# The passage from three attention layers to a state space layer: banks, load order and diagonals

## The chip, the cores and the metric

The kernel runs on one core of one Trainium2 chip. The metric is the device time of one launch in microseconds (us), the median of several runs. Engines are named as in the profile: PE (TensorE matmul) and PEld (its weight loads), DVE (VectorE), ACT (ScalarE), POOL (GpSimd), and SP (SyncE), which here issues nearly all DMAs.

## The reference

Four layers run one after the other over x of shape (8, 512, 256), all conditioned by `cond`. Layers 0 to 2 are transformer blocks (attention and an MLP). Layer 3 is a bidirectional state space layer with a gated MLP. Cut to the part that matters:

```python
def _mamba(h, ...):
    x, z = jnp.split(h @ in_proj_W, 2, axis=-1)              # 512 channels each
    x = silu(causal_conv(x, conv_w) + conv_b)                # 4 taps per channel
    xdbl = x @ x_proj_W                                      # 16 + 32 + 32 columns
    dt = softplus(xdbl[..., :16] @ dt_proj_W + dt_proj_b)
    Bm, Cm = xdbl[..., 16:48], xdbl[..., 48:]
    A = -jnp.exp(A_log)
    # for each time t, for 512 channels x 32 states:
    #   hst = hst * exp(dt_t * A) + dt_t * B_t * x_t ;   y_t = sum_n hst * C_t
    return (ys + Dp * x) * silu(z) @ out_proj_W
h = ln(x) * (1 + s1) + sh1
x = x + g1 * (mamba(h) + flip(mamba(flip(h))))
x = x + g2 * (silu(h2 @ w1) * (h2 @ w2) @ w3)                # h2: the second norm of x
```

All data is float32.

## The kernel before

The activations are kept transposed: 128 channels on the partitions, 512 time steps along the free axis. Layers 0 to 2 share one set of pools and hand their results over through DRAM (`x_mid`). When their pools close, those of layer 3 open in the same memory.

Every engine's order of work is the order in which the Python code emits it. Each engine takes its own list in order and waits with semaphores, so the order written by hand is the schedule.

**Layer 3** makes 16 steps: for each of 8 batch items a forward and a reversed pass. A step's preparation is `prep3`; a step's recurrence is `recur`, 64 turns k of 32 channels by 8 states (c = k // 16 is the channel block, gp = k % 16 // 4 the pair of state groups, j = k % 4). In a turn:

- `fill(k)` (L1190, PE): 64 small products of the transposed inputs `ut` with the diagonal matrices `dg` write one `bx` tile, two PSUM banks wide. There are three `bx` tiles, which take six of the eight banks; one bank each goes to `bank` and to `yc`.
- `decay(k)` (L1165, ACT): two exponentials into `da`, of which there are four (`N_DA`). They read `dtr`, the step size of 32 channels copied to four groups of partitions.
- `scan(k)` (L1204, DVE): two scans of 128x512. After each second turn POOL multiplies by `cs` (L1208), and PE sums over the states into `yc` (L1229 to L1236).

The preparation of later steps is interleaved with the turns by credits. The preparation of the first step has nothing beside it: `run_interleaved(prep3(*steps[0]))`. It runs through these places, all of which put PE's products into the one `bank` tile:

- `norm3`: mean (L883) and variance (L892), with DVE, ACT and POOL work between (L885, L888, L893, L895, L897, L900).
- four products with `w_x0` (L861), copied out by ACT (L954);
- `convolve`: four times three products (L930), finished by DVE (L937), then a silu on ACT (L964);
- the product with `w_x` (L971), copied out twice (L973, L975); transposes (L982) to `bt` (L986);
- four products with `w_dt` (L996), each copied out by ACT (L999); one softplus (L1002);
- `dt` goes to DRAM in `dt_s` (L1005), from where `spread` (L1115) fetches `dtr`; C goes through `c_s`, from where `spread_c` (L1123) fetches `cs`;
- four times: a POOL product `uc` (L1011; one buffer), four transposes (L1019), a copy to `ut` (L1023).

After it come `spread_c` and `diagonal` for all four gp. A diagonal of one s is 8 ACT instructions (L1138) or one POOL instruction (L1142), after `DIAG = "AAPA"`. Only then `recur` begins, which first calls `spread` for four q.

The setup ahead of `prep3` loads `w_x`, `w_dt`, four pieces of `a_log` (made into `negA` on ACT, L818), `w_x0` (`fetch`, L797) and last the input `hz` (L877).

Of the kernel before, what the change touches and what calls it, by code (L numbers as in the profile page):

```python
# [7 lines left out]
F32 = mybir.dt.float32  # L8
# [6 lines left out]
B, L, D = 8, 512, 256  # L15
N_STATE, D_IN, DT_RANK = 32, 512, 16
# [12 lines left out]
SUMS_LATE, DIAG, STAGGER, RATE, CREDIT = 3, "AAPA", 2, 4.0, 4.0  # L29
# [38 lines left out]
def run_interleaved(*gens):  # L68
    live = list(gens)
    while live:  # L70
        live = [g for g in live if next(g, "end") != "end"]
# [3 lines left out]
def dit_mamba_kernel(ctx: ExitStack, tc: tile.TileContext, t, out):  # L75
    nc = tc.nc
# [13 lines left out]
    def vcol(name, i):  # L90
# [6 lines left out]
    x_mid = {  # L97
        (l, b): dram.tile([D, L], F32, tag=f"xm{l}_{b}", name="x_mid") for l in range(3) for b in range(B)
    }
# [20 lines left out]
    with ExitStack() as actx:  # L120
# [4 lines left out]
        def bank():  # L125
            return ps.tile([128, L], F32, tag="s", name="s", bufs=7)
# [645 lines left out]
    with ExitStack() as mctx:  # L772
        mp_ = mctx.enter_context(tc.tile_pool(name="mp", bufs=1))
        scr = mctx.enter_context(tc.tile_pool(name="scr", bufs=2, space=bass.MemoryType.DRAM))
        ps_m = mctx.enter_context(tc.tile_pool(name="ps_m", bufs=1, space=PSUM))

        def bank():
            return ps_m.tile([128, L], F32, tag="bank", name="bank")

        order = ["w_x0"]
# [4 lines left out]
        def fetch(name, tag="wp", bufs=1):  # L787
            w = mp_.tile([128, 1024], F32, tag=tag, name="w", bufs=bufs)
            if name in ("w_x0", "w_z0"):
                src, k = t["w_in"].rearrange("(k p) m -> p k m", p=128), 2  # L790
                src = src[:, :, 0:D_IN] if name == "w_x0" else src[:, :, D_IN:]
            else:
                k = t[name].shape[0] // 128
                src = t[name].rearrange("(k p) m -> p k m", p=128)
            m = src.shape[-1]
            ring[name] = w[:, 0 : k * m].rearrange("p (k m) -> p k m", k=k)
            nc.sync.dma_start(ring[name], src)  # L797
# [9 lines left out]
                fetch(order[0])  # L807

        w_x = mp_.tile([128, 4, 80], F32, tag="w_x", name="w_x")
        nc.sync.dma_start(w_x, t["w_x"].rearrange("(k p) m -> p k m", p=128))  # L810
        w_dt = mp_.tile([80, D_IN], F32, tag="w_dt", name="w_dt")
        nc.sync.dma_start(w_dt[64:80, :], t["w_dt"])
        negA = mp_.tile([128, N_Q, N_G], F32, tag="negA", name="negA")
        a_log = mp_.tile([128, N_Q, N_STATE], F32, tag="ut", name="a_log", bufs=N_UT)
# [24 lines left out]
        xp = mp_.tile([128, 4, L + 6], F32, tag="xp", name="xp")  # L839
        nc.vector.memset(xp[:, :, 0:3], 0.0)  # L840
        nc.vector.memset(xp[:, :, L + 3 : L + 6], 0.0)
        fetch(order[0])


        WAIT, LAST, ALONE = -1, 100, 200
        st = {}
        n_p = N_G // 2
        n_k = N_Q * n_p

# [5 lines left out]
        def dense(w, src, n_k, c):  # L855

            p = yield from free_bank()
            for k in range(n_k):
                if k == 2:
                    yield 2  # L860
                nc.tensor.matmul(  # L861
                    p, w[:, k, c * 128 : (c + 1) * 128], src[:, k, :], start=k == 0, stop=k == n_k - 1
                )
            return p

        def free_bank():
            while held[0]:
                yield WAIT
            held[0] = True
            return bank()  # L870

        def taken():
            held[0] = False

        def load_x3(b, tag):
            x = st[tag, b] = mp_.tile([128, 2, L], F32, tag=tag, name=tag)
            nc.sync.dma_start(x, x_mid[2, b].rearrange("(k p) n -> p k n", p=128))  # L877

        def norm3(x, h, sq, r, sc, sh):

# [61 lines left out]
        def prep3(b, rev):  # L942

            if not rev:
# [7 lines left out]
                for c in range(4):  # L952
                    p = yield from dense(w, h, 2, c)
# [13 lines left out]
            p = yield from free_bank()  # L967
# [12 lines left out]
            p = yield from free_bank()  # L980
# [10 lines left out]
            dt_s = scr.tile([D_IN, L], F32, tag="dt", name="dt_s")  # L991
            st["in", b, rev] = us, uts, dt_s, c_s
            dt = mp_.tile([128, 4, L], F32, tag="dt", name="dt")
            for c in range(4):
                p = yield from free_bank()
# [6 lines left out]
            nc.scalar.activation(dt, dt, AF.Softplus)  # L1002
            use_exp_ln(pin=False)
            yield ALONE
            nc.sync.dma_start(dt_s.rearrange("(c p) t -> p c t", p=128), dt)  # L1005
            st["dt", b, rev] = True

            def transposed(c):
# [19 lines left out]
            live, c, i = [], 0, 0  # L1028
            while live or c < 4:
# [4 lines left out]
                for g in list(live):  # L1034
                    n = next(g, None)
                    while n == WAIT:
                        yield WAIT
                        n = next(g, None)
# [62 lines left out]
        def later(turns, fn):  # L1101
            todo.append([turns, fn])
            todo.sort(key=lambda e: e[0])
# [3 lines left out]
        def spread(step, q):  # L1107

            if (step, q) in dtr:
                return  # L1110
            dt_s = st[("in",) + step][2]
            rt = mp_.tile([128, L], F32, tag="dtr", name="dtr", bufs=N_DT)
            src = dt_s[32 * q : 32 * q + 32, :]
            for n in range(4):
                nc.sync.dma_start(rt[32 * n : 32 * n + 32, :], src)  # L1115
            dtr[step, q] = rt

        def spread_c(step, gp):

            w = mp_.tile([128, 2, L], F32, tag="cs", name="cs", bufs=n_p)  # L1120
            src = st[("in",) + step][3].rearrange("(g n) t -> n g t", n=4)
            for n in range(4):
                nc.sync.dma_start(  # L1123
                    w[32 * n : 32 * n + 32, :, :],
                    src[n : n + 1, 2 * gp : 2 * gp + 2, :].to_broadcast([32, 2, L]),
                )
            cs[step, gp] = w

        def diagonal(step, gp, s):

            if s == 0:
                dg[step, gp] = mp_.tile([128, 4, 4, 64, 2], F32, tag="dg", name="dg", bufs=n_p)
            o = dg[step, gp][:, s]
            bt = st[("bt",) + step][:, s, 8 * gp : 8 * gp + 8]
            if DIAG[s] == "A":
                for i in range(2):
                    for n in range(4):
                        nc.scalar.activation(  # L1138
                            o[:, n, :, i], eye, AF.Copy, scale=bt[:, 4 * i + n : 4 * i + n + 1]
                        )  # L1140
            else:
                (nc.vector if DIAG[s] == "V" else nc.gpsimd).tensor_tensor(  # L1142
                    o, eye[:, None, :, None].to_broadcast([128, 4, 64, 2]),
                    bt.rearrange("p (i n) -> p n i", i=2)[:, :, None, :].to_broadcast([128, 4, 64, 2]),
                    ALU.mult,
                )
# [22 lines left out]
        def recur(step, nxt, ys):  # L1169
# [75 lines left out]
            for k in range(n_k):  # L1245
                c, gp, j = k // 16, k % 16 // 4, k % 4
                run_due(1)
                if k % 2 == 0:
                    fill(k)
                    fill(k + 1)  # L1250
                    for i in range(0 if k else -AHEAD, 2):
                        decay(step, nxt, k + AHEAD + i)
                n_ut[1] += k % 16 == 15
                later(2, lambda k=k: scan(k))
                if j == 3:
                    later(2 + SUMS_LATE, lambda c=c, gp=gp: sums(c, gp))
                    if c == 3 and nxt:
                        for s in range(4):
                            later(1 + 3 * s, lambda gp=gp, s=s: diagonal(nxt, gp, s))
                        later(4, lambda gp=gp: spread_c(nxt, gp))  # L1260
                if k % 16 in SPREAD:
                    i = SPREAD.index(k % 16)
                    if c < 3:
                        spread(step, 4 * (c + 1) + i)
                    elif nxt and ("dt",) + nxt in st:
                        spread(nxt, i)
                yield k
# [9 lines left out]
        steps = [(b, rev) for b in range(B) for rev in (False, True)]  # L1277

        def before(step):

            b, rev = step
            if rev:
                conv = convolve(b, True)
                if b:

                    for _ in range(6):
                        yield next(conv)
                    while (b - 1, True) not in done:
                        yield WAIT
                yield from conv  # L1290
                yield from gates(b)
                if b + 1 < B:
                    load_x3(b + 1, "hz")
            yield from prep3(b, rev)

        def behind(b, ys):

            while (b, True) not in done:
                yield WAIT
            yield from project(b, ys)  # L1300

            yield from mlp3(b, ys[:, 2:4, :])
            
            if b + 1 < B:
                load_x3(b + 1, "x")
                fetch("w_out", "wq", 1)

        load_x3(0, "hz")
        run_interleaved(prep3(*steps[0]))
        for gp in range(n_p):  # L1310
            spread_c(steps[0], gp)
            for s in range(4):
                diagonal(steps[0], gp, s)
        ys = mp_.tile([128, 4, L], F32, tag="ys", name="ys")
        load_x3(0, "x")
        fetch("w_out", "wq", 1)
# [1 line left out]
        for i, step in enumerate(steps):  # L1318
            b, rev = step
# [137 lines left out]
```

## Time and profile before

| | |
|---|---|
| median of three runs | 6478.48 us (6462.92, 6478.48, 6481.08) |
| the profiled execution | 6473.94 us |
| its span, first to last instruction | 6472.1 us |
| busy share of the span | PE 90%, DVE 64%, POOL 57%, ACT 54% |
| mean granted TensorE clock | 0.959 |
| last store of layer 2 (L748) issued | 3455.11 us after the span's start |
| first product of layer 3 (L883) | 3467.19 us |
| first decay, first scan | 3564.09 us, 3564.82 us |

In timeline rows the columns are start (us), length (us), engine, line, operation, output and inputs, shape, count, and in brackets the idle time of the engine ahead and what ended it. Several instructions are merged into one row. A float32 product of 128x512 is two PE rows, called passes here.

### The profile page before, as it was taken

The page shows a single profiled execution, that of the slowest core. Times are in us where ns is not written, and L with a number is a line of the kernel's source. Part 1 is how long each engine was busy: PE and PEld are TensorE (multiplying, and loading weights), DVE is VectorE, ACT ScalarE, POOL GpSimd, SP SyncE. Part 2 cuts the span into 40 slices and gives each one's busy share as a digit, 9 for nine tenths or more (in the row PEclk, how much of TensorE's full clock was granted, in tenths as well). Part 3 has the DMA queues.
Part 4 walks back from the last instruction along what each step waited for, and adds up shares of the span by engine and source line. Part 5 has one row for each costly group of instructions (what it writes and reads, how often), then busy time and mean ns, then how long its engine had stood idle before and what let it go on. Part 6 is the DMA issues. An engine that isn't in the chain of part 4 may idle for free.

```text
span 6472.1 us, 200572 instructions
## 1 busy us (share of the span) xinstructions
PE 5842.6 (90%) x88928; PEld 2917.0 (45%) x88928; DVE 4110.2 (64%) x5102; ACT 3513.7 (54%) x6855; POOL 3665.9 (57%) x1464
## 2 busy tenths in 40 slices
PE   8999999999999989999995888988888888888887
PEld 4333335555555544333332444444444444444443
DVE  4554545544554544455531887888878888888886
ACT  2444444333433433444443677777777677777773
POOL 1110126655556662111001888888989888988896
PEclk8999999999999999999997999999999999999999
DMA  2001101000000000101001111112121211111120
GB/s 86 24 25 28 32 21 37 24 27 27 17 27 27 27 14 24 41 26 26 24 12 51 39 49 54 58 56 62 52 65 51 67 43 59 60 53 57 49 64 24
DMA packets 168559, 260.31 MB, mean 40 GB/s; under 512 B 40448, under 2 KB 58368, under 8 KB 167696
## 3 DMA queue, kind: packets, MB, share of 16 engines
q1 hardware_dynamic: 167152, 246.44, 12.5%
q8 instruction: 702, 11.50, 0.7%
q14 instruction: 161, 1.32, 0.1%
q10 hardware_dynamic: 544, 1.05, 0.0%
HBM read 186.53 MB, written 34.60 MB: 34 GB/s over the span
## 4 chain that ended last, share of the span: by engine, by line
PE 68%; ACT 10%; POOL 9%; DVE 6%; issue 5%; DMA 1%; SPq 1%; POOLq 0%; DVEq 0%; ACTq 0%
PE s L381 10%; PE s L674 8%; PE bx L1190 8%; POOL hs L1208 5%; PE bank L861 5%; PE s L637 5%; PE s L587 5%; PE yc L1236 5%; DVE hs L1204 4%; PE o L607 3%; PE s L498 3%; PE o L538 3%; ACT da L1165 3%; PE s L528 3%; PE bank L930 3%
## 5 line engine op out<-in xcount | busy, mean ns | idle before, releaser
L1204 DVE TENSOR_TENSOR_SCAN hs<-da,bx 128x512 f32<-128x512 f32 x2048 | 2311.1, 1198 | 425.3 <-ACT da L1165 245.7
L1208 POOL TENSOR_TENSOR hs<-hs,cs 128x2048 f32<-128x2048 f32 x512 | 2323.7, 4564 | 278.1 <-DVE hs L1204 201.7
L1165 ACT ACTIVATE da<-dtr,negA 128x512 f32<-128x512 f32 x2048 | 1335.4, 713 | 260.6 <-DVE hs L1204 247.9
L1190 PE MATMUL bx<-dg,ut 64*32 64x128 f32 x65536 | 1123.4, 276 | 249.1 <-DVE hs L1204 154.3
L1190 PEld LDWEIGHTS bx<-dg,ut 64*32 64x32 f32 x65536 | 941.8, 107 | 655.9 <-issue 473.9
L519 POOL TENSOR_SCALAR pr<-pr,sums 128x512 f32<-128x512 f32 x512 | 796.5, 1575 | 571.2 <-DVE sums L517 570.7
L592 DVE TENSOR_REDUCE negp<-s 128x1 f32<-128x512 f32 x1024 | 637.6, 683 | 586.7 <-PE s L587 586.2
L643 ACT ACTIVATE pt<-s 128x512 f32<-128x512 f32 x1024 | 527.7, 601 | 440.4 <-PE s L637 440.3
L1236 PE MATMUL yc<-hs,r 128*32 128x512 f32 x4096 | 608.1, 637 | 82.4 <-POOL hs L1208 81.4
L510 ACT ACTIVATE pr<-s,negm 128x512 f32<-128x512 f32 x512 | 345.1, 686 | 300.1 <-DVE negm L509 286.5
L529 DVE COPY pt<-s 128x512 f32<-128x512 f32 x512 | 321.6, 683 | 192.2 <-PE s L528 178.5
L509 DVE TENSOR_REDUCE negm<-s 128x1 f32<-128x512 f32 x512 | 317.4, 682 | 142.3 <-PE s L498 142.2
L587 PE MATMUL s<-kT,qT 32*128 32x512 f32 x2048 | 368.7, 653 | 36.1 <-ACT pt L643 18.2
L674 PE MATMUL s<-g,w_w 128*128 128x512 f32 x768 | 361.7, 617 | 23.9 <-ACT g L738 14.6
L1138 ACT ACTIVATE dg<-eye,bt 128x64 f32<-128x64 f32 x1536 | 381.3, 342 | 0.3 <-PE bx L1190 0.3
L353 POOL TENSOR_TENSOR xs<-x 128x512 f32<-128x512 f32 x48 | 61.0, 1272 | 564.1 <-DVE x L663 181.6
L381 PE MATMUL s<-h,w_w 128*128 128x512 f32 x768 | 366.5, 618 | 13.9 <-POOL h L372 13.9
L381 PE MATMUL s<-h,wqkv 128*128 128x512 f32 x768 | 368.3, 615 | 4.9 <-POOL h L372 4.7
L700 POOL COPY wide<-rec 128x1024 f32<-128x1024 f32 x16 | 16.6, 1037 | 622.9 <-DVE rec L698 622.9
L637 PE MATMUL s<-q,kT 32*128 32x512 f32 x2048 | 366.3, 649 | 1.8 <-DVE qs L454 1.4
L1236 PEld LDWEIGHTS yc<-hs,r 128*32 128x32 f32 x4096 | 126.7, 113 | 459.9 <-issue 297.9
L528 PE MATMUL s<-base,pr 128*128 128x128 f32 x2048 | 263.7, 279 | 42.9 <-POOL pr L519 37.9
(166 smaller groups left out, 6265.2 us busy)
## 6 DMA issues: line engine op xcount, KB each, us to landing
dtr<-dt_s SPq DMA_DIRECT2D x1024, 64.0 KB
cs<-c_s SPq DMA_DIRECT2D x256, 128.0 KB
wqkv<-in_wqkv_dram SPq DMA_DIRECT2D x48, 512.0 KB
dt_s<-dt SPq DMA_DIRECT2D x16, 1024.0 KB
x_mid<-x SPq DMA_DIRECT2D x24, 512.0 KB
x<-x_mid SPq DMA_DIRECT2D x24, 512.0 KB
w<-in_w_g_dram SPq DMA_DIRECT2D x24, 384.0 KB
qT<-qs SPq DMA_DIRECT2D x256, 32.0 KB
```

Of the source, the lines that this page charges most:

```text
L381: nc.tensor.matmul(p, w[:, k, o : o + 128], src[:, k, :], start=k == 0, stop=k == n - 1)
L519: nc.gpsimd.tensor_scalar(p[:, j, :], p[:, j, :], sums[:, j : j + 1], None, ALU.mult)
L587: nc.tensor.matmul(ss[j], u.qT[r, c, qt * 128 : (qt + 1) * 128], u.kT[r, c, :], start=True, stop=True)
L592: nc.vector.tensor_reduce(negp[c % 2][:, qt, i : i + 1], ss[j], AX.X, ALU.max, negate=True)
L637: nc.tensor.matmul(ss[j], u.kT[r, c, i * 128 : (i + 1) * 128], q2[u, c][r, :], start=True, stop=True)
L643: nc.scalar.activation(pt[j // 2][:, j % 2, :], ss[j], AF.Exp)
L674: nc.tensor.matmul(p, w[:, first + c, m * 128 : (m + 1) * 128], srcs[c], start=c == 0, stop=c == n - 1)
L1165: nc.scalar.activation(da[:, i, :], dtr[step, 4 * c + j], AF.Exp, scale=negA[:, 4 * c + j, g : g + 1])
L1190: nc.tensor.matmul(bx[k][32 * n : 32 * n + 32, r, 128 * s : 128 * s + 128], uts[c][64 * r : 64 * r + 64, s, 32 * j : 32 * j + 32], d[64 * ...
L1204: nc.vector.tensor_tensor_scan(h, back(da[:, i, :]), back(x[:, i, :]), 0.0, ALU.mult, ALU.add)
L1208: nc.gpsimd.tensor_tensor(hs[t_], hs[t_], cs[step, k % 16 // 4][:, None, :, :].to_broadcast([128, 2, 2, L]), ALU.mult,)
L1236: nc.tensor.matmul(yc[c][32 * j : 32 * j + 32, :], r32, h[j // 2][:, j % 2, i, :], start=False, stop=gp == n_p - 1 and i == 1, tile_positi ...
```

## The change

It touches four things, all in the passage from layer 2 to the first recurrence step, and leaves all instructions after the first ten turns in their order.

1. While the first preparation is alone, `bank()` hands out the first half of a `bx` tile, three in turn, in place of the one `bank` tile.
2. The first input `hz` and then `w_x0` are the first DMAs of layer 3; `w_x`, `w_dt` and `a_log` follow.
3. `dt` of the first step goes to DRAM in four pieces, and the 16 DMAs of `dtr` are issued ahead of the 16 of `cs` instead of behind them.
4. The diagonals of the first gp are made by DVE (s = 0, 2) and ACT (s = 1, 3); those of the other three gp keep `DIAG`, but are emitted during turns 0 to 9 instead of ahead of the recurrence.

In each engine's list before and after: ACT had 96 diagonal instructions, then decays; it now has 32, the decays of turns 0 and 1, 8, two turns of decays, 16, two turns, 8, two turns, 16, two turns, 8. POOL's four diagonals become three, between its multiplications. DVE has two more instructions, ahead of its first scan. ACT's four `negA` instructions now stand between those of the norm: one ahead of L888, two ahead of L893, one ahead of L900.

```diff
+        alone = [True]
         def bank():
+            if alone[0]:
+                return ps_m.tile([128, 2, L], F32, tag="bx", name="bank", bufs=3)[:, 0, :]
             return ps_m.tile([128, L], F32, tag="bank", name="bank")
...
+        load_x3(0, "hz")
+        fetch(order[0])
         nc.sync.dma_start(w_x, t["w_x"].rearrange("(k p) m -> p k m", p=128))
...
-        fetch(order[0])
...
-            nc.sync.dma_start(dt_s.rearrange("(c p) t -> p c t", p=128), dt)
+            for cs_ in [slice(c, c + 1) for c in range(4)] if alone[0] else [slice(0, 4)]:
+                nc.sync.dma_start(
+                    dt_s.rearrange("(c p) t -> p c t", p=128)[:, cs_, :], dt[:, cs_, :]
+                )
...
-        def diagonal(step, gp, s):
+        def diagonal(step, gp, s, on=None):
...
-            if DIAG[s] == "A":
+            on = on or DIAG[s]
+            if on == "A":
...
-        load_x3(0, "hz")
         run_interleaved(prep3(*steps[0]))
+        alone[0] = False
+        for q in range(4):
+            spread(steps[0], q)
         for gp in range(n_p):
             spread_c(steps[0], gp)
             for s in range(4):
-                diagonal(steps[0], gp, s)
+                if gp == 0:
+                    diagonal(steps[0], gp, s, "VAVA"[s])
+                else:
+                    later(4 * gp - 3 + s // 2, lambda gp=gp, s=s: diagonal(steps[0], gp, s))
```

More of the change, by code (lines that the diff above doesn't have):

```diff
@@ L809, in dit_mamba_kernel, with load_x3 @@
         w_x = mp_.tile([128, 4, 80], F32, tag="w_x", name="w_x")
+        w_dt = mp_.tile([80, D_IN], F32, tag="w_dt", name="w_dt")
+        st = {}
+        def load_x3(b, tag):
+            x = st[tag, b] = mp_.tile([128, 2, L], F32, tag=tag, name=tag)
+            nc.sync.dma_start(x, x_mid[2, b].rearrange("(k p) n -> p k n", p=128))
+        load_x3(0, "hz")
+        fetch(order[0])
         nc.sync.dma_start(w_x, t["w_x"].rearrange("(k p) m -> p k m", p=128))
-        w_dt = mp_.tile([80, D_IN], F32, tag="w_dt", name="w_dt")
         nc.sync.dma_start(w_dt[64:80, :], t["w_dt"])
@@ L841, in dit_mamba_kernel @@
         nc.vector.memset(xp[:, :, L + 3 : L + 6], 0.0)
-        fetch(order[0])
         WAIT, LAST, ALONE = -1, 100, 200
-        st = {}
         n_p = N_G // 2
@@ L873, in taken @@
             held[0] = False
-        def load_x3(b, tag):
-            x = st[tag, b] = mp_.tile([128, 2, L], F32, tag=tag, name=tag)
-            nc.sync.dma_start(x, x_mid[2, b].rearrange("(k p) n -> p k n", p=128))
         def norm3(x, h, sq, r, sc, sh):
@@ L1141, in diagonal @@
             else:
-                (nc.vector if DIAG[s] == "V" else nc.gpsimd).tensor_tensor(
+                (nc.vector if on == "V" else nc.gpsimd).tensor_tensor(
                     o, eye[:, None, :, None].to_broadcast([128, 4, 64, 2]),
```

## The prediction

> **What bounds the kernel now.** I read three views: the chain of work that ended last, in order of time, over the passage (3455 to 3600 us); the timeline of each engine there; the clock by windows. Outside the passage the change leaves every list as it is, so a shift of the first recurrence step moves the whole rest with it. The chain, thinned (start, us, what):
>
> ```profile
> 3455.11 2.73 DMA x_mid<-x
> ...
> 3461.58 5.48 DMA hz<-x_mid
> 3467.19 3.36 PE bank L883 x4
> ...
> 3481.05 3.80 PE bank L861 x4
> 3484.87 0.59 ACT xp L954
> 3485.51 3.79 PE bank L861 x4
> ...
> 3497.08 2.86 PE bank L930 x6
> 3500.03 0.76 DVE u L937
> 3500.83 2.86 PE bank L930 x6
> ...
> 3512.13 3.65 PE bank L971 x8
> ...
> 3517.69 1.14 PE bank L996 x2
> 3518.85 0.70 ACT dt L999
> ...
> 3540.70 0.59 ACT ut L1023
> 3541.28 20.08 ACT dg L1138 x85
> ```
>
> To see: a load that is issued late and takes twice as long as a store of the same 512 KB; then PE and the engine that empties the one bank taking turns; then ACT alone with the diagonals. The timelines of ACT and PE show where that ends:
>
> ```profile
> 3541.18 23.01 ACT L1138 ACTIVATE dg<-eye,bt 128x64 f32<-128x64 f32 x96
> 3564.09 8.06 ACT L1165 ACTIVATE da<-dtr,negA 128x512 f32<-128x512 f32 x13
> ...
> 3567.30 1.97 PE L1190 MATMUL bx<-dg,ut 64*32 64x128 f32 x64 [14.42 <-DVE hs L1204]
> ```
>
> ACT goes from diagonals to decays with no idle time, so nothing but its own list held the first decay; PE had filled all three banks and waited 14.42 us.
>
> The clock (busy times by engine, then PEclk, DMA share, GB/s), and PE's weight loads in a product of layer 2 that has enough banks:
>
> ```profile
> 3485.50:3490.00 4.50, 3.82 (x5) 1.21 (x5) 0.00 (x0) 0.59 (x1) 0.00 (x0) 0.50 0.00 0
> 3501.00:3512.00 11.00, 8.36 (x18) 2.99 (x18) 2.21 (x3) 1.98 (x3) 0.00 (x0) 1.00 0.00 0
> ...
> 3441.80 0.34 PEld L674 LDWEIGHTS s<-g,w_w 128*128 128x128 f32 x1 [0.52 <-issue]
> 3442.66 0.21 PEld L674 LDWEIGHTS s<-g,w_w 128*128 128x128 f32 x1 [0.52 <-issue]
> 3443.11 0.19 PEld L674 LDWEIGHTS s<-g,w_w 128*128 128x128 f32 x1 [0.24 <-issue]
> ```
>
> At clock 0.50 a pass of 512 columns takes 0.855 us, at 1.00 it takes 0.43. Layer 2's last two series of 32 passes without a pause started at half clock and turned to full after 5 passes (3414.89, L381) and 7 (3436.52, L674). L861's products, with a pause of 0.68 us after every four passes, took the longer time in twelve.
>
> **Part 1, the load order.** SP could issue layer 3's first DMA at 3458.03; `hz` had seven ahead of it and came at 3461.58. It now goes first: 3.55 us earlier. The landing took 5.48 us behind 0.9 MB, the store of equal size 2.73; first in line I take the store's. PE then starts at 3458.03 + 2.73 + 0.1 = 3460.9, 6.3 earlier; I book **6.1**, 0.2 less for `w_x0` close behind (between 3.5, if the landing stays long, and 6.3). What was moved past: `a_log` comes behind 1.2 MB, and ACT's first `negA` now stands ahead of the norm's square. That is ready at 3460.9 + 3.4 (L883) + 1.3 (L885) = 3465.6. 1.2 MB at the 212 GB/s of 3461 to 3465 us take 5.7 us: `a_log` lands near 3464 to 3466. Booked at nothing; without cover 1 to 2 us. The norm itself is one chain over four engines, 13.86 us, in which no bank is waited for: unchanged.
>
> **Part 2, the banks.** L861 to the first L930 took 16.03 us. With three banks the 16 passes run on. Six at half clock and ten at full (between the 5 and 7 above): 6 x 0.855 + 10 x 0.43 = 9.4, gain **6.6** (8 at half clock: 5.7; 4: 7.4). L930 to L971 took 15.05; 24 passes of 0.43 are 10.3, gain **4.7**. The silu of the last `u` (0.75 + 0.72) lies under the first six passes of L971 (2.6), so L971's 3.65 stays, and so do the copies after it.
>
> L996: the first starts after the transposes, at 3517.25 in before's time, in place of 3517.69; 8 passes of 0.43 + 0.26 end at 3520.95, the last copy at 3521.75 instead of 3527.14: gain **5.4**. If the clock falls as it did at 3521 (windows: 0.52 from 3521 to 3525), 8 passes of 0.95 leave 1.4. I take the first, since the stage now ends before the point at which the clock fell. Softplus (3.2 us) and the four rounds of `uc`, transposes and `ut` (10.8 us) stay: there the chain runs through POOL's one `uc` buffer, not through the bank.
>
> [...]
>
> **Part 3, the diagonals and DMAs.** From the last `ut` (3541.29) to the first decay were 22.80 us: 96 instructions at 23.01 / 96 = 0.24. Now 32 stand ahead: 7.7. Gain **15.1**. The two on DVE need only `bt` (3517.65). The trace has no such DVE instruction; the nearest row, 128x512 with one PSUM input (L601), takes 0.68, POOL's own 1.23: 1.4 to 2.5 us for two, inside 52.79 us in which DVE had nothing to do.
>
> The other 56 (13.4 us) now lie between decays, and hold those queued behind them on ACT. Counted from the first decay, with 0.64 per decay, the exponentials of turn 8 end at 23.1 where DVE could begin its scan at 22.1 and use the first half at 22.4; the other turns are ready before DVE is. ACT reaches the copy `zs` (L914) at 28.9; before it stood there at 27.85, and PE's next product waits for it. Loss **1.0** (0 to 3). POOL's two late diagonals (1.23 each) fall into its idle times of 2.06 and 1.89.
>
> `dtr`: the first piece of `dt_s` (256 KB) should land within the 2.73 of 512 KB; 16 issues at 0.59 (row L1123: 9.39 for 16) end 12.7 us after the softplus, and the first decay comes at 10.9 + 7.7 = 18.6. `cs`'s first four are issued by 15.1 and, with a landing as long as 5.5, are there at 20.6; POOL asks for them at 24.6. Both are covered by at least 4 us; each us beyond would count in full.
>
> **Sum.** 6.1 + 6.6 + 4.7 + 5.4 + 15.1 - 1.0 = 36.9 us. Against the profiled execution's 6473.94 (span 6472.1 and 1.8 around it) that gives 6437.0; the median of the runs shown lies 4.5 higher, so the forecast for a median is 6478.5 - 36.9 = **6441.6**.
>
> **Rivals.**
>
> *ACT becomes the bound of the first turns.* If decays must wait for the diagonals between them in full, because a late scan holds `bx`, PE's list and so the next scan, the 13.4 us come back in place of the 1.0 booked: 36.9 + 1.0 - 13.4 = 24.5 saved, 6454. For it: ACT's work there is not less than DVE's. Against: ACT had 17 us of idle time in those 40, waiting for DVE and PE.
>
> *The clock stays at half through the passage.* Then L861's 16 passes take 13.7 (gain 2.3), L930's 24 take 20.5 (loss 5.5), L971 7.2 (loss 3.6), L996 gains 1.4: 22.1 less than booked, 14.8 saved, 6463.7. Against: layer 2's unpaused series turned to the full clock. [...]
>
> *Slower: the recurrence runs at a lower clock.* [...] PE is busy 2499.6 us of 3565 to 6472 at 0.96, with 0.93 to 0.98 by stretches of 180 us. At 0.92, with PE's 68% of the chain, it costs 2499.6 x (0.96 / 0.92 - 1) x 0.68 = 74 us: 6515. It eats the whole gain from 0.94 down. Against: the same list of instructions, only shifted.
>
> *The change does not do what it says* I give nothing of its own: PE's waits in the built kernel no longer name the copy ahead.
>
> **Numbers.** Forecast 0.85, ACT as bound 0.07, clock at half in the passage 0.05, lower clock in the recurrence 0.03. The unknowns at their low ends save 3.5 + 5.7 + 4.7 + 1.4 + 15.1 - 3.0 = 27.4, at their high ends 6.3 + 7.4 + 4.7 + 5.4 + 15.1 = 38.9; the runs scatter by 18 us, 9 to each side: 6478.5 - 38.9 - 9 = 6431 to 6478.5 - 27.4 + 9 = 6460. It takes in the first rival and leaves out the other two. A measurement of this kernel tells about 0.3% (19 us, the scatter of its runs) from no change: faster is below 6459. Of the forecast 0.82 lies there and 0.03 above, of the first rival 0.04 and 0.03; the second rival is within: faster 0.86, same 0.11, slower 0.03.
>
> **What would show it.** First L883 near 3461; L861 to L930 in 9 to 10 us with the clock turning after four to eight passes; L930's rows following each other with no DVE between; L996 done within 4.5 us of its start; first decay about 7.7 us after the last `ut`, near 3526 instead of 3564; scans of turns 0 to 11 in about 32 us, as before. Wrong, if ACT's first `negA` holds the square, if the decays show idle time ended by a DMA, if PE stays at 0.50 through L930, or if the first scan is early by some 38 us and the span is not.

## The result and the profile after

| | before | after |
|---|---|---|
| median of the runs compared | 6476.9 us (4 runs) | 6435.7 us (6422.8 to 6438.2, 4 runs) |
| profiled execution, its span | 6473.94 us, 6472.1 us | 6435.02 us, 6433.2 us |
| mean granted clock | 0.959 | 0.960 |

The ratio is 0.9944 (95% interval 0.993 to 0.9957): the changed kernel is faster, by 41 us in the medians and 38.9 us in the profiled spans. The forecast was 6441.6 us.

Layers 0 to 2 are untouched, but layer 2's last store (`x_mid<-x`, with which the passage begins) was issued at 3455.11 us before and at 3452.67 us after. All distances here are therefore counted from that store. The 2.44 us between the two belong to no edit; in the twelve traces of this case that store lies anywhere from 3451.96 to 3461.43 us.

The chain of waits after, in order of time (start, us, what), thinned to the rows that answer to those of before:

```profile
3452.67 2.74 DMA x_mid<-x
...
3459.38 3.77 PE bank L890 x4
...
3474.08 8.96 PE bank L872 x16
3483.04 10.30 PE bank L937 x24
3493.34 3.45 PE bank L978 x8
...
3498.53 3.18 PE bank L1003 x7
3501.73 0.69 ACT dt L1006
```

Where PE and an emptying engine took turns, there are now three PE rows end to end: 16, 24 and 8 passes with no ACT or DVE between them. ACT's timeline, and the clock by windows over the `w_x0` products:

```profile
3516.46 7.75 ACT L1150 ACTIVATE dg<-eye,bt 128x64 f32<-128x64 f32 x32
3524.10 2.54 ACT L1177 ACTIVATE da<-dtr,negA 128x512 f32<-128x512 f32 x4
3526.55 2.01 ACT L1150 ACTIVATE dg<-eye,bt 128x64 f32<-128x64 f32 x8
...
3474.00:3478.00 4.00, 3.92 (x5) 1.77 (x6) 0.00 (x0) 0.83 (x3) 0.00 (x0) 0.53 0.00 0
3478.00:3483.00 5.00, 5.00 (x13) 2.21 (x12) 0.00 (x0) 1.65 (x3) 0.00 (x0) 1.00 0.00 0
```

32 diagonals in 7.75 us stand ahead of the first decay instead of 96 in 23.01; eight more follow behind the decays of turns 0 and 1. The clock (the eighth figure of a window's row) turned to full in the fifth pass and stayed there.

Stage by stage, between the same events in both traces:

| stage | before | after | change | predicted |
|---|---|---|---|---|
| store to first layer 3 product | 12.08 | 6.71 | -5.37 | -6.1 |
| norm, to first `w_x0` product | 13.86 | 14.70 | +0.84 | 0 |
| `w_x0`, to first convolution product | 16.03 | 8.80 | -7.23 | -6.6 |
| convolution, to first `w_x` product | 15.05 | 10.30 | -4.75 | -4.7 |
| `w_x` and `w_dt`, to last copy of `dt` | 15.01 | 9.24 | -5.77 | -5.4 |
| softplus and transposes, to last `ut` | 14.15 | 14.13 | -0.02 | 0 |
| last `ut` to first decay | 22.80 | 7.55 | -15.25 | -15.1 |
| **store to first decay** | **108.98** | **71.43** | **-37.55** | **-37.9** |
| first decay to the copy `zs` | 27.85 | 28.09 | +0.24 | +1.0 |

The first scan of turn 12 comes 142.55 us after the store before and 105.20 after: 37.35 us earlier. With the 2.44 ahead of the store that is 39.8 of the span's 38.9. The missing 0.9 us went in the later steps. That it was so little is chance: from the first decay to the end two traces of the same changed kernel took 2909.1 and 2893.9 us.

### The profile page after: what moved, and what is told of

It is laid out like the page before. It is cut to its first block, busy times and chain, and to the rows that moved or that the text cites. A ratio compares the mean times of both kernels' runs of the same rounds, so it can differ in the third digit from the quotient of the medians.

```text
span 6433.2 us, 200570 instructions
## 1 busy us (share of the span) xinstructions
PE 5845.2 (91%) x88928; PEld 2917.9 (45%) x88928; DVE 4113.7 (64%) x5104; ACT 3509.2 (55%) x6847; POOL 3663.6 (57%) x1463
## 4 chain that ended last, share of the span: by engine, by line
PE 67%; ACT 10%; POOL 10%; DVE 6%; issue 5%; DMA 1%; SPq 1%; POOLq 0%; DVEq 0%; ACTq 0%
PE s L381 10%; PE s L674 8%; PE bx L1202 8%; POOL hs L1220 6%; PE bank L872 5%; PE s L637 5%; PE yc L1248 5%; PE s L587 4%; DVE hs L1216 4%; PE o L607 3%; ACT da L1177 3%; PE s L498 3%; PE o L538 3%; PE s L528 3%; PE bank L937 2%
```

## The experiments

Stage lengths repeat from trace to trace within about 0.2 us, unless the clock falls otherwise; whole times scatter by 11 to 29 us within one kernel that was timed. So the verdicts below rest on stages, and the ratios (against the kernel before, in the same comparison) stand beside them.

| kernel | store to first decay | median (runs) | ratio, 95% |
|---|---|---|---|
| after | 71.43 | 6435.7 (4) | 0.9944 (0.993 to 0.9957) |
| one bank | 86.63 | 6459.4 (10) | 0.9974 (0.9964 to 0.9984) |
| diagonals ahead | 89.21 | 6454.7 (6) | 0.9964 (0.9951 to 0.9978) |
| old load order | 79.07 | 6446.1 (4) | 0.995 (0.9933 to 0.9966) |
| old DMA order | 72.26 | 6440.8 (4) | 0.9945 (0.9931 to 0.996) |
| one bank, PE kept busy | 83.08 | 6442.3 (1) | one run |
| PE kept busy | 67.66 | 6443.1 (4) | 0.994 (0.9925 to 0.9955) |
| all diagonals on DVE | 66.26 | 6433.9 (4) | 0.9923 (0.9907 to 0.994) |
| the same, old DMA order | 72.14 | 6441.6 (1) | one run |
| last version | 60.33 | 6420.3 (5) | 0.9915 (0.9902 to 0.9927) |
| after, run beside it | 71.40 | 6436.0 (6) | 0.9935 (0.9922 to 0.9948) |

**1. One bank.** Three of the four edits stay; `bank()` hands out the one tile again.

```diff
-            if alone[0]:
-                return ps_m.tile([128, 2, L], F32, tag="bx", name="bank", bufs=3)[:, 0, :]
```

> The changed kernel with the one bank tile again during the first preparation; load order, DMA order and diagonals stay changed. Distances count from the issue of layer 2's last store to the first decay: 109.0 us before, 71.4 us after. Theory (the three banks take away the wait for each copy, and so PE's pauses that kept the clock at half): the products with w_x0, the convolution and the products with w_dt go back to 16.0, 15.0 and 15.0 us; the first decay comes at 71.4 + 17.7 = 89.1 us, the time at 6435.7 + 17.7 = 6453 us. [...]

The first decay came 86.63 us after the store: 15.2 us of the 37.5 went, where the theory had 17.7. The convolution was back at 15.05 us exactly. The stage of `w_x` and `w_dt` took 15.94 us, against 15.01 before. The `w_x0` stage took 12.40 us, not before's 16.03. Its PE rows:

```profile
3473.69 3.74 PE L870 MATMUL bank<-hz,w 128*128 128x512 f32 x4 [4.76 <-ACT hz L905]
3478.11 1.98 PE L870 MATMUL bank<-hz,w 128*128 128x512 f32 x4 [0.68 <-ACT xp L959]
```

The pause of 0.68 us after every four passes, which ACT's copy ends, is there as before. But this time the clock turned to full after the first four passes (3.74 us, then 1.98), where before it stayed at half through the first twelve. The wait for the bank is certain; what the clock adds to it depends on the run. The median lies 23.7 us above after's; the stages explain 15.2 of that, and the rest is spread over later steps in which the two kernels do the same.

**2. Diagonals ahead.** All 16 are made ahead of the recurrence, by the engines of before.

```diff
-                if gp == 0:
-                    diagonal(steps[0], gp, s, "VAVA"[s])
-                else:
-                    later(4 * gp - 3 + s // 2, lambda gp=gp, s=s: diagonal(steps[0], gp, s))
+                diagonal(steps[0], gp, s)
```

> The changed kernel with all 16 diagonals of the first step ahead of the recurrence again, shared out as in the old list; banks, load order and DMA order stay changed. Theory (ACT's list alone held the first decay, and its idle time in the first turns takes the diagonals between decays): first decay 22.8 us after the last ut instead of 7.6, at 86.7 us from layer 2's last store; the turns after it take as long as before; time 6435.7 + 15.0 = 6451 us. Rival (ACT bounds the first turns, so that the diagonals between decays are paid there): first decay equally late, but the copy zs comes only 2 to 5 us later than in the changed kernel, time 6438 to 6441 us.

ACT's timeline:

```profile
3525.55 23.00 ACT L1150 ACTIVATE dg<-eye,bt 128x64 f32<-128x64 f32 x96
3548.45 8.05 ACT L1177 ACTIVATE da<-dtr,negA 128x512 f32<-128x512 f32 x13
```

Last `ut` to first decay was 22.80 us again, as before to the hundredth. From the first decay to the copy `zs` took 28.36 us, against 28.09 in after: with all diagonals ahead, the first turns ran no faster. So the 56 that lie between the decays cost nothing there, and the rival in which ACT becomes the bound falls. (The other 2.5 us in this kernel's 89.21 come from the clock: `w_x0` and `w_dt` passes at half clock, 10.04 us for 16 and 5.18 for 7, cost 3.3, and the norm took 0.85 less.)

**3. Old load order.** `w_x`, `w_dt`, `a_log` and `w_x0` first, `hz` last.

```diff
-        load_x3(0, "hz")
-        fetch(order[0])
...
+        fetch(order[0])
+        load_x3(0, "hz")
```

> The changed kernel with the old order of the first loads (the input last); banks, DMA order and diagonals stay changed. Theory: first product of layer 3 at 12.1 us after the last store instead of 6.7, of which 3.5 us are the issue and 1.9 the landing; the norm's four passes that the changed kernel ran at half clock may come back 0.8 us; time 6435.7 + 4.5 to 5.4 = 6440 to 6441 us. Rival (the landing takes 5.5 us wherever the load stands, so only the issue counts): first product at 10.3 us, time 6439 us.

```profile
3465.29 3.43 PE L890 MATMUL bank<-hz,base 128*128 128x512 f32 x4 [13.45 <-DMA hz<-x_mid]
```

PE's row shows the releaser, the load. The product came 11.91 us after the store, 5.20 later than in after. The first decay moved by 7.64: these 5.20, less 0.84 for the norm (its products at before's 3.4 us), and 3.3 more for `w_x0` and `w_dt` passes that met the half clock.

**4. Old DMA order.** `dt` goes out in one piece, and `dtr` is issued behind `cs`.

```diff
-            for cs_ in [slice(c, c + 1) for c in range(4)] if alone[0] else [slice(0, 4)]:
+            for cs_ in [slice(0, 4)]:
...
-        for q in range(4):
-            spread(steps[0], q)
```

> The changed kernel with dt stored in one piece and the copies of dt fetched behind those of C, as before; banks, load order and diagonals stay changed. Theory (both are covered by the transposes and the 32 diagonals): the fetches of turn 0 are issued from about 11 us after the softplus and land some 2.7 us later, about 3 us ahead of the first decay; nothing moves, first decay at 71.4 us, 6436 us. Rival (the order was needed): ACT shows idle time ended by a DMA ahead of its first decays, first decay 2 to 6 us later, 6438 to 6442 us.

```profile
3533.38 2.56 ACT L1177 ACTIVATE da<-dtr,negA 128x512 f32<-128x512 f32 x4 [1.70 <-DMA dtr<-dt_s]
```

My theory was nothing; the decays waited 1.70 us for `dtr`. With 32 diagonals ahead of them in place of 96, the old order is no longer covered: the new one is worth 1.7 us as soon as part 3 is in. (The first decay moved by only 0.83 us, since in this trace the norm and the `w_x0` passes took 1.1 less than in after.)

The four parts undone singly lose 15.2, 15.25, 5.2 and 1.7 us in their own stages: 37.4, against 37.5 gained. That the two agree so well is chance. The banks' three stages gained 17.75 us in the change, and run 1 gave back less because its clock turned earlier than before's; and the 1.7 of the DMA order have no part in the 37.5, since without part 3 the old order cost nothing.

**5. One bank, PE kept busy.** To part the two halves of the bank's cost, the clock and the wait, PE gets products into a tile that nobody reads, in its pauses.

```diff
-            if alone[0]:
-                return ps_m.tile([128, 2, L], F32, tag="bx", name="bank", bufs=3)[:, 0, :]
...
+        def warm(n):
+            for _ in range(n if alone[0] else 0):
+                nc.tensor.matmul(wm[:, 0:256], ident, base, start=True, stop=True)
```

> The kernel with one bank during the first preparation, and with products added in PE's pauses there (a constant with itself, 256 columns, into the yc bank, read by nobody): 6, 3 and 8 around the two products of the norm, 1 or 2 behind each product with w_x0, the convolution and w_dt, 9 behind the last of these, 2 behind each group of transposes. The waits for the copies stay, the pauses that PE sees do not. Theory (of the 7.1 us that the banks gained at the products with w_x0, some 3 were the wait and the rest the clock): every product with w_x0 takes 1.98 us and the four 10.6 us to the convolution (16.0 before, 12.4 in the run with one bank, 9.0 with three); the convolution keeps its 15.0 us, which were at full clock already; the products with w_dt come every 1.9 us. Rival (the clock does not follow PE's work within a few us): the mean and the variance take 3.7 us each and the first products with w_x0 3.7 us, as without the added products.

```profile
3475.87 1.98 PE L870 MATMUL bank<-hz,w 128*128 128x512 f32 x4 [1.32 <-ACT hz L914]
3478.53 1.98 PE L870 MATMUL bank<-hz,w 128*128 128x512 f32 x4 [0.24 <-ACT xp L970]
```

Four rounds at full clock, 2.66 us apart, took 10.64 us. Of before's 16.03, 5.4 us were the clock, and the waits for the bank are 10.64 less the 6.97 that three banks take at full clock (next run): 3.7 us. `w_dt` went to half clock here (two passes took 2.07 us from the third on, 1.12 before that) although PE had hardly a pause in it.

**6. PE kept busy.** The same products (6 ahead of the mean's, 3 behind them, 8 behind the variance's, 2 behind those of `w_x`, 9 behind those of `w_dt`, 2 in each round of the transposes), in the changed kernel.

> The changed kernel with the same added products in PE's remaining pauses (6, 3 and 8 around the two products of the norm, 2 and 9 around those with w_dt, 2 behind each group of transposes). Theory (the clock turns after some 5 us of unbroken work and stays while PE works): mean and variance 2.0 us each instead of 3.75, the 16 passes with w_x0 in 7.1 instead of 9.0 us, each group of transposes in 0.6 instead of 1.12 us: first decay 7.5 us earlier, 64 us from layer 2's last store, time 6428 us. Rival (the added products stand in front of the needed ones in PE's list and cost what they gain): first decay between 69 and 73 us, time 6434 to 6438 us.

```profile
3480.92 7.13 PE L872 MATMUL bank<-hz,w 128*128 128x512 f32 x16 [1.32 <-ACT hz L916]
```

`w_x0` took 6.97 us to the convolution instead of 8.80, the variance's products 1.99 instead of 3.8, and the first decay came 3.8 us earlier, not the 7 hoped for. The theory's "some 5 us" lie between the 4.3 and 6.0 us (5 and 7 passes of 0.855) after which layer 2's two series turned before the change. The mean's products stayed at half clock (3.65); the six ahead of them ran at once, and PE then idled for 4.58 us. In run 9 it idled for 2.06 us behind twelve, and they took 3.64. The nine behind `w_dt` took 6.61 us and held the first transposes by 1.0. The median did not fall: 3.8 us is less than these runs' scatter.

**7. All diagonals on DVE.** DVE had nothing to do for 25 us there; could it spare ACT's 7.75?

```diff
-                if gp == 0:
-                    diagonal(steps[0], gp, s, "VAVA"[s])
-                else:
-                    later(4 * gp - 3 + s // 2, lambda gp=gp, s=s: diagonal(steps[0], gp, s))
+                diagonal(steps[0], gp, s, "V")
```

> The changed kernel with all 16 diagonals of the first step on DVE, ahead of its first scan, where it sits idle for 25 us. Theory (the 32 diagonals on ACT are all that separates the last ut from the first decay, and dt has landed by then): 16 of 0.64 us are done 10.3 us after bt, the first decay follows the last ut at once, 7.6 us earlier, at 63.9 us from layer 2's last store; no diagonal stands between decays; time 6428 us. Rival (the fetches of C come too late for POOL's first multiplication, or DVE's work slows POOL's beside it): decays early by 7.6 us, but the second half of the first 12 turns no more than 4 us early; time 6432 us or above.

DVE's and POOL's timelines:

```profile
3501.79 9.73 DVE L1154 TENSOR_TENSOR dg<-eye,bt 128x512 f32<-128x512 f32 x16 [4.49 <-ACT bt L993]
3508.88 3.77 POOL L1022 TENSOR_TENSOR uc<-u,dt 128x512 f32<-128x512 f32 x1 [32.63 <-ACT dt L1009]
3523.62 2.33 DVE L1216 TENSOR_TENSOR_SCAN hs<-da,bx 128x512 f32<-128x512 f32 x2 [12.10 <-PE bx L1202]
```

The first decay came right behind the last `ut`, 5.2 us earlier than in after; 2.5 of the 7.7 were lost because POOL's first `uc` took 3.77 us in place of 1.26. The first scan of turn 12 came only 2.0 us earlier. DVE now waits for PE, whose list runs from the last transposes to the product that `zs` copies with no wait but one of 1.75 us that the profile doesn't explain; its first two fills ran at half clock (3.98 us, against 2.03 for the next two). The diagonals are off the path, and PE is next.

**8. The same, with the old DMA order of run 4.**

> The kernel with all 16 diagonals on DVE, but with dt stored in one piece and fetched behind C, as before. In the run with the old DMA order the first decay waited 1.70 us for a fetch of dt and came 9.3 us after the last ut. Theory (the order of the DMAs is worth only what the diagonals no longer cover): the first decay waits for the fetch and again comes 9.3 us after the last ut, in place of 0 to 1; time 9 us above that of the kernel with all diagonals on DVE. Rival (the wait came from traffic that moves along): first decay within 3 us of the last ut.

```profile
3530.04 2.56 ACT L1177 ACTIVATE da<-dtr,negA 128x512 f32<-128x512 f32 x4 [5.76 <-DMA dtr<-dt_s]
```

The first decay waits 5.76 us for `dtr`, and comes 5.9 later than in run 7. The theory had 9.3 us after the last `ut`; but that `ut` itself came 2.5 us later here than in run 4, behind the slow `uc`, and the fetch 1.1 earlier, counted from the softplus. One edit, three prices: without part 3, 23 us of diagonals cover the old order; with part 3 it costs 1.7 us; with no diagonals on ACT, 5.9.

**9. The last version.** The added products of run 6 with other counts (12, 3, 8, 2, 7, 2); the diagonals where they cost least: ten on DVE, four on POOL behind its last `uc`, two on ACT between decays.

```diff
+                if gp < 3 or s < 2:
+                    diagonal(steps[0], gp, s, ("VVVV", "VVVV", "VVPP", "PP")[gp][s])
                 else:
+                    later(5 + s, lambda gp=gp, s=s: diagonal(steps[0], gp, s, "A"))
```

> The changed kernel with two additions. The first step's diagonals: ten on DVE (gp 0, 1 and half of gp 2; 6.1 us, done before POOL's first uc), four on POOL behind its uc (4.9 us, before its first multiplication), two on ACT between later decays. And the added products in PE's pauses (12, 3 and 8 around the norm's, 2 and 7 around those with w_dt, 2 behind each group of transposes). Theory (both shorten the path to the first decay, and the gain that the kernel with all diagonals on DVE lost was POOL's slowed uc, 2.5 us, and PE's fills at half clock): uc stays at 1.26 us, mean and variance 2.0 us each, the first decay follows the last ut at once, 71.4 - 7.6 - 7.0 = 57 us from layer 2's last store, the copy zs 85 us from it instead of 99.5; time 12 to 14 us below the changed kernel of the same call, some 6423 us. Rival (what is saved ahead of the first decay is given back in the first 12 turns, where PE's and POOL's lists set the pace): the copy zs above 93 us, time less than 7 us below the changed kernel.

```profile
3513.25 6.28 ACT L1189 ACTIVATE da<-dtr,negA 128x512 f32<-128x512 f32 x10
3533.39 1.02 PE L1253 MATMUL yc<-u,dp_d 128*128 128x512 f32 x2 [3.42 <-issue]
3539.14 2.33 DVE L1228 TENSOR_TENSOR_SCAN hs<-da,bx 128x512 f32<-128x512 f32 x2 [3.14 <-PE bx L1214]
3546.55 0.59 ACT L930 COPY zs<-bank 128x512 f32<-128x512 f32 x1 [9.79 <-PE bank L872]
```

The first decay came 11.1 us earlier than in after (run again beside it), the first scan of turn 12 5.8 us. Half is given back in the first turns: DVE waits for PE's `bx`, and ACT stands idle for 9.79 us ahead of `zs`, where in after it had no idle time. `zs` came 93.64 us after the store, not at the 85 hoped for, as the rival has it. Whether PE's list sets that pace, as the rival says, is open: PE stood still for 3.42 us ahead of its sums, and the profile names no releaser. The medians lie 15.7 us apart; the traces account for 5.8 of that (`zs`), the two profiled executions differ the other way (6426.97 and 6419.11 us), the intervals of the two ratios overlap, and what the rest is stays open.

> The changed kernel itself, on the same chip and in the same rounds, for the comparison. Every theory: 0.994 of the kernel before, about 6436 us, first decay 71 to 74 us from layer 2's last store, by how many of the passes run at half clock.

This second profile of the changed kernel repeats the first: `w_x0` 8.84 us (8.80), first decay 71.40 (71.43), `zs` 99.48 (99.52).

## Why the prediction was right

**The step that was mis-sized: the landing of `hz`.** It was booked at 2.73 us, a store's, plus 0.2; the first product came 6.71 us after the store instead of 6.0, and the gain was 5.37 instead of 6.1. In run 1 the profile names the load as what released that product: issued at 3455.06, it landed 3.79 us later, and the product followed at 3458.99. That is 1.06 us more than the store's 2.73, not 0.2. Whether `w_x0` close behind costs this, or a load takes longer than a store in any case, no run shows. In after the profile names DVE instead:

```profile
3459.38 3.75 PE L890 MATMUL bank<-hz,base 128*128 128x512 f32 x4 [8.25 <-DVE xp L854]
```

That cannot be what the product waited for. In the second profile of the changed kernel PE began the product's weight load before the same DVE row was over (at 3458.59):

```profile
3458.52 0.07 DVE L854 MEMSET xp<- 128x12 f32 x1
3458.56 0.50 PEld L890 LDWEIGHTS bank<-hz,base 128*128 128x128 f32 x2 [8.97 <-issue]
```

The trace also records the semaphore updates of a DMA. In before and in after the product starts 0.136 us after the last update of `hz`'s load (in after 3.65 us behind its issue), while its distance from DVE's end is 5.45 us in before, 0.07 in after and 0.00 in the second profile of the changed kernel. So the load held the product in after, too; DVE's end was only close by.

**Banks: right in its three terms** (-7.23, -4.75, -5.77 against -6.6, -4.7, -5.4), and in the reason of the first two: the clock turned in the fifth pass, four to eight being the forecast, and stayed. No run shows the four and the eight, which set this term's range, as limits: with three banks and no added products the 16 passes took 8.57 us (run 4) to 10.04 us (run 2), which by 0.855 and 0.43 us for a pass I estimate at about four to seven at half clock, and before the change it was twelve. The third was in part luck. The prediction took the full clock for `w_dt` because the stage would end before the point at which the clock had fallen. In runs 2 and 3, which give PE the same list there, the clock fell all the same, and the stage took 11.3 us instead of 9.24, a gain of 3.7; run 2's row:

```profile
3505.59 5.18 PE L1003 MATMUL bank<-bcd,w_dt 16*128 16x512 f32 x7
```

The clock's turns went together in six of the seven traces with three banks and no added products: in the two traces of after and in runs 7 and 8 the norm took 14.70 us, `w_x0` 8.8 and seven passes of `w_dt` 3.16 (none of them at half clock); in runs 2 and 3 the norm took 13.85 and 13.86, `w_x0` 10.0, and in `w_dt` the clock fell (5.18 and 5.20). The passage is 2.4 us longer in the second pattern. Run 4 has neither (13.87, 8.57 and 3.28). The rival of half clock through the passage falls: 1.00 from 3478 us, and the convolution's 24 passes at 0.43. With three banks the rows of 48 passes follow each other without a gap, and the clock stays at 1.00 from 3478 to 3497 us, once it has turned.

**The norm was not unchanged:** +0.84 us. Its mean and variance products took 3.77 and 3.80 us in place of 3.36, wholly at half clock (0.50 over both). The prediction had written "unchanged" because no bank is waited for, and left out that the clock can turn elsewhere in the norm. That the earlier start did it is not shown: in runs 2 and 4, which load `hz` first too, the norm took 13.85 and 13.87 us, as before.

**Diagonals: 15.25 against 15.1**, by counting instructions ahead of the first decay. The loss between the decays was 0.24 us and not 1.0, as run 2 shows by the other side: ACT's four decays take 2.45 us from start to start (3524.10 to 3526.55), 0.61 each, where 0.64 had been booked for each of the 24 ahead of `zs`. The cover of the new DMA order held; run 7's decays, 5.2 us earlier, found `dtr` there. That the edit was needed, the prediction did not see: it priced the new order, not the old one beside 32 diagonals.

**ACT's `negA` ahead of the square** delayed nothing: the variance's input (L895) starts at 3464.43, as the subtraction ahead of it ends. **A lower clock in the recurrence** falls: 0.960 after, 0.959 before; from first decay on, the profiled executions need 2909.1 and 2908.0 us, and the second one of the changed kernel 2893.9.

The errors of +0.7, +0.84, -0.6, -0.4 and -0.8 us nearly cancel, so the sum fits better than its terms: 37.35 us saved up to turn 12, against 36.9. The median lies 5.9 us below the forecast; the passage gives 0.4 of that, and the rest lies outside it, in the 2.44 us ahead of the store and in the scatter of whole times.

## What to carry to other kernels

Between two phases, look for the one engine whose list stands ahead of the next phase's first instruction, and count what of it that instruction does not need: 64 of 96 diagonals were worth 15 us. Banks and engines that only a later phase uses are idle in the passage and can serve it. Moved work was nearly free where its engine had been idle (56 diagonals between the decays, 0.24 us), and a removed wait can uncover another's (here the order of DMAs, worth 0, 1.7 or 5.9 us); where whole times scatter by 0.3%, measure this by distances between events in the trace.

## What the runs showed of the hardware

**DVE and POOL took longer beside each other in two places.** In run 7 POOL's first `uc` took 3.77 us and ended 1.13 us after DVE's series of diagonals did (3511.52); in after, where DVE stands idle, it takes 1.26. The reverse stands in after's timeline of both:

```profile
3470.84 2.34 POOL L904 TENSOR_TENSOR hz<-hz,rstd 128x1024 f32<-128x1024 f32 x1 [57.68 <-ACT rstd L902]
...
3471.18 2.08 DVE L834 TENSOR_SCALAR negA<-negA 128x128 f32<-128x128 f32 x1 [6.79 <-ACT negA L831]
```

DVE's multiplication, 0.23 us before the change, where it is done (3463.66) before POOL's product begins (3477.81), took 2.08 here and ended just after POOL's product (3473.26 and 3473.18). In run 7 the two ran side by side for 2.64 us, some four of DVE's instructions at 0.61 us each, and POOL's product took 2.51 us more than in after. Run 8 repeats it (PE waits 7.89 us for that `uc`, 7.90 in run 7 and 5.39 in after), and in run 9, where DVE's ten diagonals end 2.46 us before POOL's first `uc` begins, that `uc` takes 1.26 us again. Why the two slow each other is not shown.

**The clock can fall while PE is busy.** In the last version, over the products of `w_dt` (16 rows of weights), PE was busy 4.00 of 4.00 us, and the granted clock was 0.65:

```profile
3496.00:3500.00 4.00, 4.00 (x7) 1.22 (x5) 4.00 (x7) 2.06 (x3) 0.00 (x0) 0.65 0.00 0
```

The seven passes that stand in one row there took 4.65 us, against 3.16 in after and in runs 7 and 8, where none ran at half clock. Some ran at half clock in before and in runs 1 and 5 (2.07 us for two, against 1.12), and in runs 2, 3 and 6 (5.18, 5.20 and 4.04 us for seven); in run 4 (3.28 us) it was part of one. The reason is open. Before the change the `w_x0` products, 3.8 us busy of each 4.46, stayed at half clock for 13 us (0.51 from 3481.0 to 3494.2); in run 1 the same pattern turned after one round (1.00 from 3478 to 3486). Whether a series with pauses gets the full clock could not be foretold from its pauses here.
